# Top-query attention, routed FFN and linear attention on one core: attention's closing stage in two groups of batches, the gate layers of linear attention in four strips and three

## The chip, the cores and the metric

The kernel runs on one NeuronCore of a Trainium2 chip. Its engines are TensorE (PE: matmuls into PSUM; its weight loads are listed apart as PEld), VectorE (DVE), ScalarE (ACT), GpSimd (POOL) and SyncE (SP, which here only issues DMAs). Each runs its own instructions in order; semaphores make one wait for another. The metric is the device time of one execution in microseconds, as a median over several runs.

## The reference

All arrays are float32. The input `x` has 8 batches of 512 tokens with 256 channels. Four sublayers follow each other, each added to `x` after a layer norm:

1. Attention with 16 heads of 16 channels, in which only the 307 queries of a head with the largest sparsity count; the output of every other query is zero.
2. A routed FFN: 16 blocks of 64 hidden units, of which each token uses the 4 that a softmax router ranks highest.
3. Gated linear attention over the batch axis (8 time steps, for each of 512 tokens), with its own RMS norms and a SwiGLU FFN.
4. The routed FFN again, with the same weights.

```python
scores = einsum('bhqd,bhkd->bhqk', q, k) * scale
sparsity = scores.max(axis=-1) - scores.mean(axis=-1)
_, top_idx = top_k(sparsity, U)                 # U = int(0.6 * 512)
...
out = zeros_like(q).at[bi, hi, top_idx].set(softmax(scores_sel) @ v)
return out @ Wo + bo
```

```python
gate_hidden = silu(xb @ wg1.T + bg1)            # 256 -> 16
alpha = sigmoid((gate_hidden @ wg2.T + bg2) / GATE_TEMP)    # 16 -> 256
S = a_t[..., None] * S + k_t[..., :, None] * v_t[..., None, :]   # S is zero before step 0
o_t = einsum('bhk,bhkv->bhv', q_t, S)
```

Because the state is zero before the first step, the decay `alpha` of step 0 (batch 0) multiplies zero.

## The kernel before

The residual `xres` stays in SBUF for the whole run: 128 partitions by 8 batches by 4 token slices of 128 by 256 channels. Names with `_ps` are PSUM tiles; PSUM has eight banks of 512 floats per partition.

**Attention.** A list `steps` (L483) has 128 entries: batch `b`, head groups `m` and `e`, and one of four blocks `k` of queries or keys. Each step is done twice. `max_one` (L415) computes scores with queries on the partitions, and DVE takes their row maximum into `mx`. `exp_one` (L429), 16 steps later (`LAG`), computes the transposed scores, ACT takes the exponential, and `weigh` (L440) multiplies by the values into `av`. The loop at L539 mixes the two: in iteration `n` the maxima of step `n` (`ahead`) and the exponentials of step `n - 16` (`here`), until the maxima end at `n = 127` and 16 iterations of exponentials are left. The maxima draw from `bank_m`, a ring of four banks; the exponentials then draw from `bank`, a ring of three.

After the four blocks of one `(b, m, e)`, `place_maxima` (L396) transposes `mx` on PE, negates it on ACT and sends it with eight small DMAs of SP: four into spare rows of the queries `q`, where the second pass uses it as the softmax shift, and four into `neg`, which collects the values for the choice of queries (a head's row has one value per query). When the last maxima are there, `top_queries` (L464) copies `neg` to `work` and on DVE removes the largest values eight at a time, in 26 rounds of `max` and `match_replace`. `take` (L449) copies a finished `av` to SBUF, sends the row of softmax sums to `den` by a DMA of ACT, and POOL puts the two head halves together in `outC[b]`.

**End of attention.** At L617 DVE takes the reciprocal of `den` for all heads, and with the mask from `work` makes `nrm`: the weight of each head and query, 16 rows per batch. PE spreads these rows over the channels by multiplying with the constant `spread`; two batches share a strip of 32 rows. Four batches of the same parity stand in four different strips, and the loop at L621 takes them one after another. DVE multiplies `outC[b]` by the result (L630), 16 instructions in all. The memory of the weights that follow (`wpool`) becomes free with the end of attention; SP issues their loads then.

**Output projection and routing.** `out_projection` (L770) has four units per token slice `k`; a unit projects two batches with `wo_a` into a bank (four matmuls of 256 columns) and DVE adds it to `xres`. `route(k, ...)` (L787) is a generator: statistics of slice `k` on DVE, normalized rows on ACT, transposes on PE to `xnT`, the router's logits, softmax, the four highest, the mask's transpose `mT_ps`, and a DMA round trip that spreads the mask. The function `between` (L702) alternates units of one list with pieces of a generator. At L1192 the four units of slice 0 come first, then the twelve units of the other slices alternate with the routing of slice 0; the first FFN follows.

The kernel's source gives the order in which instructions are made; the tile framework sets the order within each engine's queue from it, and so a unit can appear in another place than in the text.

**Linear attention.** `gla(k)` (L961) handles one slice, and its pieces alternate with FFN units. Its gate has two layers. The first, `gh_ps` (L980), has 16 outputs and 1024 tokens of the slice as two groups of 512 columns, each in a strip of 32 PSUM rows; ACT applies SiLU. The second, `al_ps` (L992), takes the 16 values and a row of ones as 32 contraction rows and produces 256 decays for 128 tokens per matmul; the two groups lie in two strips of rows. Its result `al` is used by POOL and DVE. `vm` (L671) subtracts each head's mean from the value weights `q_w`, 12 short DVE instructions that stand in the source directly after the weight loads.

Of the kernel before, what the change touches and what calls it, by code (L numbers as in the profile page):

```python
# [10 lines left out]
F32 = mybir.dt.float32  # L11
# [6 lines left out]
P = 128  # L18
# [20 lines left out]
def block_kernel(ctx: ExitStack, tc: tile.TileContext, t: dict, out: bass.AP):  # L39
# [59 lines left out]
    with ExitStack() as outer:  # L99
# [21 lines left out]
        mx = a_out.tile([P, NB, NG, 4 * 4], F32, name="mx")  # L121
        work = a_out.tile([P, L + 8], F32, name="work")
        m8 = a_out.tile([P, 8], F32, name="m8")

        with ExitStack() as inner:
# [4 lines left out]
            def load_heads(name, src, eng):  # L130
                wp = load_chunked(a1, name + "_pad", src, eng)
# [264 lines left out]
            def place_maxima(b, m, e):  # L396


                q = fronts[b][0][e]
                pt = bank_m(f"mxT_ps{b}")  # L400
                nc.tensor.transpose(pt[0:16, 0:P], mx[:, b, 2 * e + m, :], ident)
                negT = a2.tile([16, P], F32, tag="negT", name=f"negT{b}")
                nc.scalar.mul(negT, pt[0:16, 0:P], -1.0)
                r = b * H + 8 * e + 4 * m
                for k in range(4):
                    nc.sync.dma_start(
                        out=q[DH * (1 - e) :: 32, m, bass.ts(k, P)],
                        in_=negT[4 * k : 4 * k + 4, :],
                    )
                for k in range(4):  # L410
                    nc.sync.dma_start(
                        out=neg[r : r + 4, bass.ts(k, P)], in_=negT[4 * k : 4 * k + 4, :]
                    )
# [68 lines left out]

            steps = [  # L483
# [54 lines left out]

            for n in range(len(steps) + LAG + 1):  # L539
                ahead = steps[n] if n < len(steps) else None  # L540
# [28 lines left out]
                if ahead is not None and ahead[3] == 3:  # L569
                    full.append((n + 2, ahead[0:3]))  # L570
                if n + 1 == len(steps):
                    place_full(n + 2)
                    top_queries()
# [22 lines left out]


# [15 lines left out]
        with tc.tile_pool(name="a_tail", bufs=2) as tail:  # L613

            nrm = tail.tile([P, L], F32, tag="nrm", name="nrm", bufs=1)
            rden = tail.tile([P, L], F32, tag="rden", name="rden", bufs=1)
            nc.vector.reciprocal(rden, den)  # L617
            nc.vector.scalar_tensor_tensor(
                nrm, work[:, 0:L][:, ::-1], REPL, rden, ALU.not_equal, ALU.mult
            )  # L620
            for u in range(2):  # L621
                for m in range(NC2):
                    for i in range(4):
                        b = 2 * i + u
                        rows = bass.ts(i, 32)
                        ps = (bank if i % 2 else bank_m)(f"nrm_ps{b}")
                        nc.tensor.matmul(
                            ps, spread[rows, u, m, :], nrm[rows, :], start=True, stop=True
                        )
                        nc.vector.tensor_tensor(  # L630
                            outC[b][:, m, :], outC[b][:, m, :], ps, ALU.mult
                        )

# [11 lines left out]
    q_wg2 = wpool.tile([64, D], F32, name="q_wg2")  # L647
    q_bg1 = wpool.tile([64, 1], F32, name="q_bg1")
    gh = wpool.tile([64, 512], F32, name="gh")
# [6 lines left out]
    for g in range(2):  # L656
        r = 32 * g + DH
        nc.sync.dma_start(out=q_wg2[32 * g : r, :], in_=t["b_wg2T"])
# [4 lines left out]
        nc.sync.dma_start(out=q_bg1[32 * g : r, :], in_=t["b_bg1c"])  # L663
# [6 lines left out]

    vm = wpool.tile([P, NC2, H], F32, name="vm")  # L671
    for c in range(NC2):
        for m in range(NC2):
# [597 lines left out]
```

## Time and profile before

| | us |
|---|---|
| median of 3 runs (1651.06 to 1651.93) | 1651.34 |
| the profiled execution, device time | 1653.55 |
| its span in the trace | 1651.8 |
| PE busy | 1599.0 (97%) |
| DVE busy | 969.4 (59%) |
| ACT busy | 671.7 (41%) |
| POOL busy | 334.3 (20%) |

A busy PE is not PE at its peak, because matmuls are pipelined and their ends are modelled. A float32 matmul appears as two records. In the profile's rows "a<-b" means that tile `a` is written from `b`; "x8" is a number of instructions; a bracket with an arrow names the idle time before an instruction and what ended it. The granted clock (PEclk) is the share of full TensorE speed.

Operations that the change touches, from the trace of this execution:

| operation | engine | count | length of one |
|---|---|---|---|
| row maximum (L425) | DVE | 512 | 0.68 us, one each 0.65 |
| exponential (L437) | ACT | 512 | 0.60 us |
| issue of a `neg` or `q` DMA | SP | 256 | 0.6 us |
| reciprocal of `den` (L617) | DVE | 1 | 3.34 us |
| multiply of `outC` (L630) | DVE | 16 | 0.68 us, one each 0.60 |
| projection unit `ao_ps` (8 records) | PE | 16 | 1.73 us at full clock |
| add of two FFN biases to `xres` (L797) | POOL | 32 | 1.27 us |
| SiLU of `gh` (L989) | ACT | 8 | 0.68 us |
| sigmoid of `al` (L1003) | ACT | 16 | 0.60 us |

### The profile page before, as it was taken

What the parts mean: (1) busy time and instruction counts of PE and PEld (TensorE: products, weight loads), DVE (VectorE), ACT (ScalarE), POOL (GpSimd) and SP (SyncE); (2) the same over time, 40 slices, a digit from 0 to 9 for tenths busy, and PEclk for the clock granted to TensorE, in tenths of its full rate; (3) what the DMA queues carried; (4) which work ended last, traced back from release to release, by engine and by line L of the source; (5) the groups of instructions that cost most, each with busy time, mean ns of one, the idle gap of its engine ahead of it and who ended that gap; (6) DMA issues with size and microseconds to landing.
All of it is one profiled execution on the core that took longest, in us unless ns stands there. A gap on an engine that the chain in (4) does not pass through costs nothing.

```text
span 1651.8 us, 19680 instructions
## 1 busy us (share of the span) xinstructions
PE 1599.0 (97%) x7378; PEld 820.1 (50%) x7378; DVE 969.4 (59%) x2015; ACT 671.7 (41%) x1208; POOL 334.3 (20%) x381
## 2 busy tenths in 40 slices
PE   7999999999999969999989999999999999999999
PEld 3323223333233237655564556555555556766666
DVE  6978776676667786447672666277355633344342
ACT  2366666665656814252346123622521352121010
POOL 3111111010000102114342442154223421000000
PEclk9999999999999979999999999999999999999999
DMA  3100000000000051010000001000000010011100
GB/s 109 40 2 3 2 2 3 2 2 3 2 3 3 2 165 26 3 37 13 1 1 0 1 1 27 0 0 1 0 1 1 0 26 1 20 33 35 43 26 26
DMA packets 24276, 27.58 MB, mean 17 GB/s; under 512 B 6229, under 2 KB 20725, under 8 KB 24181
## 3 DMA queue, kind: packets, MB, share of 16 engines
q1 hardware_dynamic: 23108, 24.75, 5.2%
q10 hardware_dynamic: 1072, 1.57, 0.3%
q8 instruction: 58, 0.95, 0.2%
q14 instruction: 38, 0.30, 0.1%
HBM read 21.20 MB, written 4.33 MB: 15 GB/s over the span
## 4 chain that ended last, share of the span: by engine, by line
PE 77%; DVE 14%; ACT 3%; POOL 3%; issue 1%; DMA 1%; SPq 0%; ACTq 0%; POOLq 0%; DVEq 0%
PE y_ps L889 16%; PE h_ps L909 11%; PE s L433 8%; PE s L422 8%; PE swi_ps L936 7%; PE proj_ps L1019 7%; PE av L442 7%; DVE pr L1052 2%; DVE pr L1042 2%; PE ao_ps L775 2%; PE q_ps L316 2%; PE gla_y L1144 2%; DVE mx L425 2%; PE v_ps L376 2%; PE k_ps L316 2%; POOL o L1069 1%
## 5 line engine op out<-in xcount | busy, mean ns | idle before, releaser
L425 DVE TENSOR_REDUCE mx<-s 128x1 f32<-128x512 f32 x512 | 329.0, 684 | 129.8 <-PE s L433 83.0
L437 ACT ACTIVATE e<-s 128x512 f32<-128x512 f32 x512 | 276.1, 599 | 179.0 <-PE s L433 103.5
L422 PE MATMUL s<-k,q 32*128 32x512 f32 x1024 | 298.9, 641 | 3.2 <-ACT k L367 2.5
L433 PE MATMUL s<-q,k 32*128 32x512 f32 x1024 | 294.3, 638 | 0.4 <-DVE mx L425 0.3
L889 PE MATMUL y_ps<-w,h 128*128 128x256 f32 x1024 | 232.9, 383 | 2.9 <-DVE h L918 2.9
L909 PE MATMUL h_ps<-xnT,w 128*128 128x512 f32 x512 | 229.8, 597 | 4.1 <-ACT h L917 4.1
L889 PEld LDWEIGHTS y_ps<-w,h 128*128 128x128 f32 x1024 | 194.1, 192 | 41.0 <-issue 10.8
L909 PEld LDWEIGHTS h_ps<-xnT,w 128*128 128x128 f32 x512 | 95.5, 191 | 113.8 <-issue 107.1
L442 PE MATMUL av<-e,va 128*32 128x512 f32 (+1 forms) x1120 | 141.9, 568 | 3.8 <-ACT e L437 2.4
L918 DVE TENSOR_TENSOR h<-h,mk 128x512 f32<-128x512 f32 x128 | 97.6, 774 | 78.9 <-ACT h L917 70.0
L917 ACT ACTIVATE h<-h_ps,b 128x512 f32<-128x512 f32 x96 | 65.6, 684 | 178.1 <-PE h_ps L909 178.0
L422 PEld LDWEIGHTS s<-k,q 32*128 32x128 f32 x1024 | 89.5, 184 | 86.0 <-DVE mx L425 56.1
L433 PEld LDWEIGHTS s<-q,k 32*128 32x128 f32 x1024 | 88.1, 183 | 80.8 <-ACT e L437 53.8
L894 DVE TENSOR_TENSOR xres<-xres,y_ps 128x512 f32<-128x512 f32 x48 | 32.8, 683 | 162.2 <-PE y_ps L889 125.0
L936 PE MATMUL swi_ps<-zT,w_gate 128*128 128x512 f32 x256 | 122.7, 599 | 4.8 <-DVE h L945 4.8
L936 PE MATMUL swi_ps<-zT,w_up 128*128 128x512 f32 x256 | 121.2, 594 | 0.0
L1019 PE MATMUL proj_ps<-q_w,rT 128*128 128x512 f32 x256 | 118.3, 601 | 0.0
L889 PE MATMUL y_ps<-w_down,h 128*128 128x256 f32 x512 | 116.8, 380 | 0.0
L889 PEld LDWEIGHTS y_ps<-w_down,h 128*128 128x128 f32 x512 | 95.7, 190 | 20.0 <-issue 8.5
L942 ACT ACTIVATE h<-swi_ps 128x512 f32<-128x512 f32 x64 | 38.2, 596 | 156.7 <-PE swi_ps L936 156.6
L1069 POOL TENSOR_TENSOR o<-o,pr 128x512 f32<-128x512 f32 (+2 forms) x56 | 80.9, 1444 | 58.9 <-DVE pr L1052 56.9
L797 POOL TENSOR_TENSOR xres<-xres,b 128x512 f32<-128x512 f32 x32 | 40.1, 1271 | 240.0 <-ACT row L737 217.7
(191 smaller groups left out, 1713.9 us busy)
## 6 DMA issues: line engine op xcount, KB each, us to landing
mk<-md SPq DMA_DIRECT2D x32, 256.0 KB
xres<-in_L_attn_a_x SPq DMA_DIRECT2D x8, 512.0 KB
out<-xres SPq DMA_DIRECT2D x16, 256.0 KB
q<-negT SPq DMA_DIRECT2D x128, 2.0 KB
neg<-negT SPq DMA_DIRECT2D x128, 2.0 KB
w<-in_f_w1T SPq DMA_DIRECT2D x1, 1024.0 KB
w<-in_f_w2T SPq DMA_DIRECT2D x1, 1024.0 KB
w_gate<-in_b_w_gateT SPq DMA_DIRECT2D x1, 1024.0 KB
```

What stands on the lines that cost most here:

```text
L316: nc.tensor.matmul(ps, w[:, c, bass.ts(m, P)], xnT[:, c, :], start=(c == 0), stop=(c == NC2 - 1),)
L422: nc.tensor.matmul(s, qs[e][rows, m, bass.ts(k, P)], ks[e][rows, m, :], start=True, stop=True)
L425: nc.vector.tensor_reduce(mx[:, b, 2 * e + m, r : r + 1], s, AX.X, ALU.max)
L433: nc.tensor.matmul(s, ks[e][rows, m, bass.ts(kt, P)], qs[e][rows, m, :], start=True, stop=True)
L437: nc.scalar.activation(ex, s, AF.Exp, scale=1.0 / DH**0.5)
L442: nc.tensor.matmul(av[32 * j : 32 * j + 32, queries], va[:, 8 * kt + 4 * m + j, e, :], es[j][:, queries], start=(kt == 0), stop=(kt == 3 a ...
L889: nc.tensor.matmul(y[0][:, bass.ts(i, D)], h[f][:, bass.ts(2 * u + i, P)], w[:, f, :], start=(f == 0), stop=(f == NF - 1),)
L909: nc.tensor.matmul(ps, w1[:, c, bass.ts(f, P)], xT[g][:, c, :], start=(c == 0), stop=(c == NC2 - 1),)
L918: nc.vector.tensor_tensor(hf, hf, mk[g][:, f, :], ALU.mult)
L936: nc.tensor.matmul(ps, w[:, c, bass.ts(f, P)], zT[g][:, c, :], start=(c == 0), stop=(c == NC2 - 1),)
L1019: nc.tensor.matmul(ps, rT[b // G4][:, c, bass.ts(b % G4, P)], q_w[:, c, m], start=(c == 0), stop=(c == NC2 - 1),)
L1069: nc.gpsimd.tensor_tensor(dst, dst, src, ALU.add)
```

## The change

**Maxima and placement.** A counter `coming` takes the place of `n` for the maxima. From `n = 112` on, every fourth iteration does the maxima of one more step, so that the last is done at `n = 124`; `top_queries` is then emitted there. `place_maxima` can take a part of the four query blocks: for the last `(b, m, e)` the first three go together and the fourth by itself. For the last batch the DMAs into `neg` are issued ahead of those into `q`.

```diff
+            coming = 0
+            def all_maxima(step):
+                nonlocal coming
+                coming += 1
+                if coming > len(steps) - 2:
+                    full.append((n + 1, step[0:3] + ((range(3), range(3, 4))[step[3] - 2],)))
+                elif step[3] == 3:
+                    full.append((n + 2, step[0:3]))
+                if coming == len(steps):
+                    place_full(n + 2)
+                    top_queries()
...
+                if ahead is not None:
+                    all_maxima(ahead)
+                    if n >= 112 and n % 4 == 0 and coming < len(steps):
+                        ahead = steps[coming]
+                        for i in range(4):
+                            max_one(*ahead, i, bank_m)
+                        all_maxima(ahead)
...
-                for k in range(4):
-                    nc.sync.dma_start(
-                        out=q[DH * (1 - e) :: 32, m, bass.ts(k, P)],
-                        in_=negT[4 * k : 4 * k + 4, :],
-                    )
-                for k in range(4):
-                    nc.sync.dma_start(
-                        out=neg[r : r + 4, bass.ts(k, P)], in_=negT[4 * k : 4 * k + 4, :]
-                    )
+                targets = [q[DH * (1 - e) :: 32, m, :], neg[r : r + 4, :]]
+                if b == NB - 1:
+                    targets = targets[::-1]
+                for target in targets:
+                    for i, k in enumerate(tiles):
+                        nc.sync.dma_start(
+                            out=target[:, bass.ts(k, P)], in_=negT[4 * i : 4 * i + 4, :]
+                        )
```

**Weights in two groups of batches, and eight projection units ahead.** `weights_of` does reciprocal and mask for the rows of some batches; two copies of one element on POOL make the reciprocal wait for the top-k's last `m8` and the mask for the last exponential. `weigh_outputs` is the old loop for some batches, with banks taken in turn. Batches 0 to 5 go first. Then come the weights of batches 6 and 7, six units of slices 0 and 1, the multiplies of batches 6 and 7, and two units of slice 2. These eight units (`out_unit`) use attention's banks; ACT copies the bank to SBUF and POOL adds it to `xres`. `out_projection` keeps the other eight, with DVE's add: one unit of slices 0 and 1 each, two of slice 2, four of slice 3.

```diff
+        def weights_of(batches, late, late_form):
+            rows = slice(16 * batches[0], 16 * batches[-1] + 16)
+            first = slice(rows.start, rows.start + 1)
+            nc.gpsimd.tensor_copy(rden[first, 0:1], late)
+            nc.gpsimd.tensor_copy(nrm[first, 0:1], late_form)
+            nc.vector.reciprocal(rden[rows, :], den[rows, :])
+            nc.vector.scalar_tensor_tensor(
+                nrm[rows, :], work[rows, 0:L][:, ::-1], REPL, rden[rows, :],
+                ALU.not_equal, ALU.mult,
+            )
+        def weigh_outputs(batches):
+            picks = itertools.cycle((bank, bank_m))
+            for u in range(2):
+                for m in range(NC2):
+                    for b in batches[u::2]:
+                        strip = bass.ts(b // 2, 32)
+                        ps = next(picks)(f"nrm_ps{b}")
+                        nc.tensor.matmul(
+                            ps, spread[strip, u, m, :], nrm[strip, :], start=True, stop=True
+                        )
+                        nc.vector.tensor_tensor(
+                            outC[b][:, m, :], outC[b][:, m, :], ps, ALU.mult
+                        )
+        def out_unit(tail, k, b):
+            y = bank(f"ao_ps{b}")
+            for i in range(2):
+                for m in range(NC2):
+                    nc.tensor.matmul(
+                        y[:, bass.ts(i, D)], outC[b + i][:, m, bass.ts(k, P)],
+                        wo_a[:, m, :], start=(m == 0), stop=(m == NC2 - 1),
+                    )
+            st = tail.tile([P, L], F32, tag="ao", name=f"ao{b}")
+            nc.scalar.copy(st, y)
+            x = xres[:, b : b + 2, k, :]
+            nc.gpsimd.tensor_tensor(x, x, st.rearrange("p (b d) -> p b d", d=D), ALU.add)
...
+            weights_of(range(NB - 2), m8[0:1, 0:1], last_exps)
...
+            weigh_outputs(range(NB - 2))
+            last = outC[NB - 3][0:1, 1, 0:1]
+            weights_of(range(NB - 2, NB), last, last)
+            for k in range(2):
+                for b in range(0, NB - 2, 2):
+                    out_unit(tail, k, b)
+            weigh_outputs(range(NB - 2, NB))
+            for b in (0, 2):
+                out_unit(tail, 2, b)
...
-        return [functools.partial(unit, b) for b in range(0, NB, 2)]
+        return [functools.partial(unit, b) for b in range((6, 6, 4, 0)[k], NB, 2)]
```

To make room for `nrm` and `rden`, the padded query and key weights are loaded into slots of the ring of the keys `k1` instead of tiles of their own.

**Gate layers.** The first layer has four strips of 256 columns instead of two of 512. The second takes the strips 1, 2, 3 together (six matmuls in three banks) and then strip 0, of which only batch 1 is computed; the unused decay of batch 0 is left out. `q_wg2`, `q_bg1` and `gh` have 128 rows instead of 64, with six more small loads on SP.

```diff
-        ps = bank_l("gh_ps")
+        ps = bank_l("gh_ps")[:, 0 : 2 * P]
         for c in range(NC2):
-            for g in range(2):
+            for u in range(G4):
                 nc.tensor.matmul(
-                    ps[bass.ts(g, 32), :], q_wg1[:, c, :], rT[g][:, c, :],
+                    ps[bass.ts(u, 32), :], q_wg1[:, c, :],
+                    rT[u // 2][:, c, bass.ts(u % 2, 2 * P)],
                     start=(c == 0), stop=(c == NC2 - 1),
                 )
...
+        for us in ((1, 2, 3), (0,)):
+            ps = [bank_l("al_ps") for u in us]
+            new = range(us[0] == 0, 2)
+            for i in new:
+                for y, u in zip(ps, us):
                     nc.tensor.matmul(
+                        y[:, bass.ts(i, D)], gh[bass.ts(u, 32), bass.ts(i, P)],
+                        q_wg2[bass.ts(u, 32), :], start=True, stop=True,
                     )
```

**`vm`.** Its twelve instructions move behind the first routed FFN, each group held by a one-element POOL copy (`hold`) of the newest FFN result.

## The prediction

> **What bounds the kernel now.** I read the page's slice rows first, then the chain of waits between 480 and 680 us, then stretches of 10 us there, then the tensor engine's (PE's) timeline. The slice rows:
>
> ```profile
> PE   7999999999999969999989999999999999999999
> PEclk9999999999999979999999999999999999999999
> ```
>
> PE is full nearly everywhere, so work that leaves PE is a gain where PE is the bound, and an idle PE is one too. One slice (the fifteenth, 578 to 619 us) stands out, in both rows. The chain there:
>
> ```profile
> 540.34 0.69 DVE mx L425
> ...
> 545.99 2.47 DMA neg<-negT
> 548.54 0.99 DVE work L468
> ...
> 589.25 3.34 DVE rden L617
> 592.67 0.66 DVE nrm L618
> 593.46 2.10 PE nrm_ps L627 x8
> 595.56 4.11 DVE outC L630 x7
> ...
> 606.25 14.98 PE ao_ps L775 x56
> ...
> 639.86 2.58 PE h_ps L909 x6
> ```
>
> Columns are start, length, engine, tile and line. The last maximum ends at 541.03; its placement lands at 548.5; 40.7 us of top-k on the vector engine (DVE) follow, up to 589.25; then reciprocal, mask, 16 multiplies, and only then the projections, all 16 of them ahead of the first FFN matmul. Attention itself (exponentials, `av`) ended at 582. What PE did meanwhile (stretch, length, busy us with counts for PE, PE's weight load, DVE, ACT, POOL, then granted clock, DMA share, GB/s):
>
> ```profile
> 570.00:580.00 10.00, 9.66 (x71) 2.79 (x68) 9.55 (x21) 9.04 (x19) 0.77 (x1) 1.00 0.01 3
> 580.00:590.00 10.00, 1.88 (x8) 0.28 (x4) 9.52 (x21) 2.65 (x4) 3.06 (x7) 0.71 0.13 16
> 590.00:600.00 10.00, 6.47 (x26) 2.39 (x26) 7.77 (x13) 0.00 (x0) 0.00 (x0) 0.60 1.07 326
> 600.00:610.00 10.00, 6.40 (x17) 3.62 (x16) 7.07 (x21) 0.00 (x0) 0.00 (x0) 0.74 0.53 159
> ```
>
> From 582 to 606 DVE is the bound, PE works 8.5 us in 24 and its clock falls. The later stretch that the change touches is the gate part of linear attention:
>
> ```profile
> 723.90 1.91 PE L983 MATMUL gh_ps<-rT,q_wg 128*32 128x512 f32 x8
> 728.10 1.99 PE L997 MATMUL al_ps<-q_wg,gh 32*128 32x256 f32 x12
> 730.64 1.13 PE L997 MATMUL al_ps<-q_wg,gh 32*128 32x256 f32 x4
> ```
>
> It stands between PE work without gaps, four times in the run.
>
> **Part 1: maxima ahead.** Iterations 112, 116 and 120 take one more step of maxima each; iterations 125 to 127 have exponentials alone. No instruction is added but a transpose. A mixed step lasts 3.66 us (14.66 for four, by the spacing of the `st` copies), an exponential-only step 2.40 (9.62 for four, ACT bound). An extra step costs PE at least 1.07 us (eight `s` records, 523.92 to 524.99). It also takes four banks of the ring of four that the maxima share, and the next maxima wait for DVE at 0.65 each; DVE has 10.3 us of maxima in 14.66, so room is there. Below 1.07 nothing can go; above, a whole step at 3.66 is the end. I take 1.6, near the PE row, because DVE drains the backlog inside the next step. Then the last maximum ends 3 x 3.66 - 3 x 1.6 = 6.2 us sooner, about 534.9, and attention ends 3 x (1.6 - 1.26) = 1.0 us later, about 583.
>
> **Part 2: placement.** The last step's tile goes by itself, `neg` first. Before, four `q` and four `neg` issues stood behind the last maximum (SP, 0.6 each) plus 2.5 to land: 7.5 us from maximum to `work`. Now SP still has the six issues of the three earlier tiles (about 533.6 to 537.2), then one issue 0.6 and 2.5 landing: `work` copy at 540.4 against 548.5, **8.1 us sooner**. The `q` issues come later, but `q` of that batch is read some 15 steps later.
>
> **Part 3: weights in two pieces.** Top-k now ends about 581 (589.25 less 8.1). The two one-element POOL copies hold the reciprocal behind the last `m8` and the mask behind the last exponential (583); behind the first copy in POOL's queue stand three `outC` operations of batch 7 (0.8 to 1.3 each), done by 584 instead of 575, which nobody needs before batch 7's weights. They also push POOL's memsets and so the weight loads on SP by 1 to 2 us; six small loads add about 4 us at SP before the gate weights. All these land before 626, needed after 640 or much later: nothing.
> Reciprocal of 96 rows: the row has 3.34 for 128 rows; fewer rows could make it 2.5, I take 3.34 (same length per row). With the last replacement (0.77) and mask (0.69), first `nrm` matmul at 585.7 against 593.46: **7.8 sooner**. First multiply 2.1 later, twelve at 0.60: the first projection's inputs are there after ten, 594.0. The `vm` work (12 instructions, 3 us at 0.17 to 0.29 each) no longer stands between the multiplies.
> The second reciprocal and mask (4 us, new) run on DVE from 595 to 601, under the first projections.
>
> **Part 4: eight projections early.** In before the first unit took 3.8 us (606.25 to its add at 610.07), the second 2.6, each later one 1.73: a slow clock, then full. Six units from 594.0: 3.8 + 2.6 + 4 x 1.73 = 13.3, so 607.3. *Clock, row and rule:* the Trainium skill ("TensorE: Matmul & The Clock Gate", "Why this matters for your kernels") says gaps up to about 3 us do not cost the clock. PE's gap shrinks from 11.6 to about 3, so by the rule all units run at 1.73, 2.9 us better. But the row above has the clock at 0.60 while PE was busy 6.5 in 10, paced by DVE as it will be again; I keep the slow start.
> Then four `nrm` matmuls of batches 6 and 7. Before, four batches sat in four row strips side by side; these two share one strip, so eight passes run one after another. *Second rule:* the same page ("The mechanism" of Part 3) lets a weight load overlap a running matmul only if the row group differs: 8 x (0.43 + 0.18) = 4.9 us. The trace's `y_ps` rows keep 0.215 apart with 0.19 loads in the same rows, so loads hide: 8 x 0.43 = 3.4 us (0.43 being half a 512-column pair, 0.86). I take 3.6, to 611. Two units more: 614.5 to 615. Each unit adds an ACT copy (0.6) and a POOL add (1.27), both shorter than the unit and on idle engines; DVE's statistics wait for POOL's adds and stand ahead of batch 6's multiply in DVE's order, about 1 us, hidden by PE's `nrm` passes.
> At 615 comes the unit for batches 6, 7 of token slice 0, on which routing of slice 0 waits. Here the gain shrinks: unit 1.7, add 0.7, statistics 1.0, so 618.5; then DVE's order has three adds or pairs of statistics of other slices (2.3) ahead of reciprocal and shift, and rows on ACT start at 621.7 against 620.34 before, **later**. But behind it PE now has 7 units instead of 12, and most statistics of slices 1 and 2 are done. Before, routing's logits waited for PE (631.56). Now they wait for ACT: eight rows at 0.5 and a copy (626.3), then in ACT's order a root and a row of slice 1, which needs DVE's shift (627.1), then the second copy (0.6): about 628.4. Softmax and top 4 took 7.9 us from transposed logits to `mT_ps` (634.4 to 642.27); one DVE add in it waits for the last unit, I take 6.7: mask transpose at 637.0 against 642.27, with 2 hidden units done in PE against 1.5 (0.86 us). Late next is this DVE chain: PE waits some 2 us for it. **Gain 5.4 + 0.9 = 6.3 us.**
>
> **Part 5: `vm` moved** behind the first FFN: 3 us on DVE in a stretch where it works 25 us in 60; its first use is at 731. Nothing; if it fell ahead of a mask multiply, up to 2 us.
>
> **Part 6: strips.** `gh`: 16 instead of 8 passes, of half the columns, four abreast instead of two: 1.91 becomes about 1.05 (four rounds of 0.215 and start), gain 0.85. Were strips not abreast, 3.4, a loss of 1.5; the logits (32 passes of 128 columns in 1.08, in four such strips) are nearest and speak for overlap. `al`: 14 passes instead of 16, three abreast, one unused block left out: four rounds of 0.76 (1.99 and 1.13, less their overlap) become three, gain 0.76. Against it: four `gh` activations of 256 for two of 0.68, about +0.35 on ACT, which the chain passes in the second of the four places. I take 1.1 net each, **4.5 us** (ends 2 and 6.4).
>
> **Sum.** 6.3 + 4.5 = 10.8 us. The profiled execution (1653.55, span 1651.8) would become 1642.8; it lies 2.2 above the median of 1651.34, which becomes **1640.5**.
>
> **Rivals.**
> - *The routing chain hides the early projections.* It starts no earlier (621.7), and DVE carries it; if it is as long as before, 6.3 falls to about 0 and the strips alone remain: 1646.8. For it: DVE is busy 8 to 9.5 in 10 there. Against: 8 adds leave DVE.
> - *PE stays slow (slower than before).* The early units are cut by waits, and the clock does not recover: eight units at 3.8 and `nrm` passes of twice the length are 8 x 3.8 + 6.9 = 37.3 us, against 13.3 + 3.6 + 3.5 = 20.4: +17, so 1657.5. It decides from about five of eight units slow (10.8 us). Against: in before two units sufficed to recover.
> - *The strips run one after another:* 1.5 lost four times, `al` no gain: 1651.3 - 6.3 + 6 = 1651.
> - An extra step of maxima priced as a full step (3.66) costs 6.2: 1646.7, held by the range.
>
> **How the numbers follow.** Forecast 0.62 (own range 1636 to 1645), hidden projections 0.20, strips serial 0.08, slow PE 0.10 (in part of it only some units are slow). Faster is the forecast, 0.19 of the second, 0.03 of the third and 0.02 of the fourth; no change 0.01, 0.05 and 0.02 of these. Uncertain terms: Part 1 from -1.6 to +6, slow start -2.9 to +3, chain 2 each way, strips 2 to 6.4. Range 1633.5 to 1648.5. 0.2% is 3.3 us, about what a measurement tells: faster 0.86, same 0.08, slower 0.06.
>
> **What would show it.** `work` copy near 540; first `nrm` matmul near 586; six `ao` units from 594; statistics' activation near 618.6; first `mT_ps` near 637; `gh_ps` groups near 1.05 us. Wrong if the three extra steps last over 6 us each, if the clock stays at 0.6 past 600, or if `mT_ps` comes at 642.

## The result, and the profile after

The changed kernel takes 1632.9 us (median of 4 runs: 1628.96, 1632.87, 1632.94, 1632.99) against 1651.49 for the kernel before: a ratio of 0.9881 with a 95% interval from 0.9869 to 0.9893. That is 18.6 us sooner. The forecast said 10.8 sooner, 1640.5, with a range down to 1633.5; the direction was right and the size was too small. A second set of runs of the same kernel, taken with the experiments, gave 1632.02 and a ratio of 0.9884 [0.9870, 0.9897]. The profiled execution is the fastest of the four (1628.96, span 1627.2), 4 us below its median, where the profiled execution of before lay 2 us above its own; differences between the two traces are therefore some 6 us too large in all.

First the page's slice rows of the changed kernel (40 slices, tenths of busy time and of granted clock):

```profile
PE   6999999999999999999989999999999999999999
PEclk9999999999999999999999999999999999999999
```

The fifteenth slice, 6 busy and 7 clock before, is now like its neighbours. The same place in stretches of 10 us (columns as before: length, busy us and counts of PE, weight loads, DVE, ACT and POOL, then granted clock, DMA share, GB/s), changed kernel:

```profile
580.00:590.00 10.00, 9.13 (x47) 2.62 (x42) 8.68 (x14) 2.79 (x6) 5.19 (x11) 1.00 0.01 2
590.00:600.00 10.00, 9.77 (x45) 8.29 (x45) 9.56 (x17) 2.92 (x5) 5.44 (x7) 1.00 0.95 289
600.00:610.00 10.00, 10.00 (x31) 6.51 (x30) 5.58 (x20) 1.23 (x3) 3.59 (x3) 0.83 0.33 78
```

PE works 28.9 us of these 30, where it worked 14.8 before. It is the bound here now; DVE, which was the bound, is hidden for most of the stretch. PE's own timeline (start, length, engine, line, operation, tiles, records; in brackets the idle time ahead and what ended it), changed kernel:

```profile
584.23 5.47 PE L147 MATMUL nrm_ps<-nrm,spread 32*128 32x512 f32 x24 [0.61 <-DVE nrm L135]
589.77 1.56 PE L160 MATMUL ao_ps<-wo_a,outC 128*128 128x256 f32 x6
591.56 9.33 PE L160 MATMUL ao_ps<-wo_a,outC 128*128 128x256 f32 x42 [0.23 <-DVE outC L150]
600.83 3.70 PE L147 MATMUL nrm_ps<-nrm,spread 32*128 32x512 f32 x8
604.45 5.40 PE L160 MATMUL ao_ps<-wo_a,outC 128*128 128x256 f32 x16
...
622.21 1.27 PE L853 MATMUL lg_ps<-xnT,rw 128*32 128x128 f32 x32
...
630.92 0.33 PE L904 MATMUL mT_ps<-ident,taken 128*128 128x128 f32 x1 [0.25 <-DVE taken L897]
```

The 11.59 us of idle time ahead of the first `nrm_ps` have become 0.61. The six early units (48 records) end at 600.83. The pair of units at 604.45 takes 5.40 instead of about 3.7: there the clock was at half speed for 3.4 us, the only such stretch of this stage. The mask's transpose, 642.27 before, comes at 630.92, and PE waits 0.25 for it.

The chain of waits of the changed kernel at the same place (start, length, what):

```profile
581.54 0.99 ACT e L485 x2
...
590.23 1.29 DVE outC L150 x2
591.56 9.33 PE ao_ps L160 x42
```

The 40 us of top-k are no longer in it; attention's last exponential and PE's work are. Between the first two lines the inferred chain goes over the last batch's sums and a small transfer, for which DVE's timeline shows no wait: its multiplies run without a break from 587.87 to 592.70. And the top-k still counts. DVE's timeline at the mask, changed kernel:

```profile
582.71 0.68 DVE L522 MATCH_REPLACE8 work<-m,work 128x520 f32<-128x520 f32 x1
583.49 0.69 DVE L135 SCALAR_TENSOR_TENSOR nrm<-work,rden 96x512 f32<-96x512 f32 x1
```

The reciprocal (579.42 to 582.77) is done ahead of the last replacement, which ends at 583.39; POOL's copy that announces the last exponential ends at 582.76. The two ways to the mask now end within 0.6 us of each other, the top-k's last.

The gates of linear attention, first of the four places, changed kernel:

```profile
711.62 1.07 PE L1030 MATMUL gh_ps<-rT,q_wg 128*32 128x256 f32 x16
715.41 1.14 PE L1047 MATMUL al_ps<-q_wg,gh 32*128 32x256 f32 x12
717.97 0.69 PE L1047 MATMUL al_ps<-q_wg,gh 32*128 32x256 f32 x2
```

`gh` went from 1.91 to 1.07, `al` from 3.12 (1.99 and 1.13) to 1.83.

### The profile page after: what moved, and what is told of

Same layout as the page of the kernel before. It is cut to its first block, busy times and chain, and to the rows that moved or that the text cites. A ratio compares the mean times of both kernels' runs of the same rounds, so it can differ in the third digit from the quotient of the medians.

```text
span 1627.2 us, 19790 instructions
## 1 busy us (share of the span) xinstructions
PE 1587.9 (98%) x7403; PEld 814.5 (50%) x7403; DVE 962.8 (59%) x2009; ACT 677.8 (42%) x1226; POOL 348.5 (21%) x397
## 4 chain that ended last, share of the span: by engine, by line
PE 77%; DVE 12%; ACT 4%; POOL 3%; issue 2%; DMA 1%; SPq 0%; ACTq 0%; POOLq 0%; DVEq 0%
PE y_ps L936 16%; PE h_ps L956 10%; PE s L481 9%; PE s L470 8%; PE av L490 8%; PE swi_ps L983 7%; PE proj_ps L1069 7%; DVE pr L1102 2%; DVE pr L1092 2%; PE q_ps L362 2%; PE gla_y L1194 2%; DVE mx L473 2%; PE v_ps L422 2%; PE k_ps L362 2%; PE chT_ps L793 2%
```

## Experiments

All medians below stand beside 1651.4 to 1651.8 us for the kernel before in the same runs; the ratio with its 95% interval decides. Gains and losses in us are differences of medians unless the ratio is named; a difference between two of the changed kernels carries the intervals of both ratios, together some 3 us.

| run | median us | ratio to before |
|---|---|---|
| after_again: the changed kernel once more | 1632.02 | 0.9884 [0.9870, 0.9897] |
| gates_only: before with the new gate layers | 1641.27 | 0.9942 [0.9929, 0.9956] |
| old_gates: changed, with the old gate layers | 1636.81 | 0.9914 [0.9901, 0.9928] |
| pe_busy: before, PE's gap filled | 1651.90 | 1.0007 [0.9999, 1.0015] |
| no_ahead: changed, no extra maxima steps | 1639.30 | 0.9925 [0.9912, 0.9937] |
| late_units: changed, no early units | 1641.97 | 0.9942 [0.9930, 0.9955] |
| gap3: changed, first weights 10 us later | 1643.92 | 0.9952 [0.9938, 0.9966] |
| ahead_only: before with the maxima ahead and their placing | 1652.62 | 1.0001 [0.9992, 1.0009] |
| ahead_vm: the same, and vm moved | 1647.88 | 0.9982 [0.9973, 0.9991] |
| vm_only: before with vm moved | 1649.80 | 0.9987 [0.9978, 0.9995] |
| vm_back: changed, vm at its old place | 1630.67 | 0.9870 [0.9857, 0.9884] |
| two_strips: changed, see below | 1628.50 | 0.9854 [0.9839, 0.9869] |
| gap1: changed, first weights 3.35 us later | 1637.05 | 0.9913 [0.9900, 0.9927] |
| al_pairs: changed, second layer in pairs of strips | 1632.90 | 0.9895 [0.9880, 0.9910] |
| gh_alone: before, first layer in four strips, second in pairs | 1643.06 | 0.9951 [0.9938, 0.9963] |
| al_twice: changed, second layer's products made twice | 1636.93 | 0.9915 [0.9902, 0.9929] |

### The two halves of the change

after_again has no edit. gates_only takes the gate part of the change over into the kernel before, old_gates takes it back out of the changed kernel:

```diff
-        ps = bank_l("gh_ps")                    # old_gates: the two hunks reversed
+        ps = bank_l("gh_ps")[:, 0 : 2 * P]
...
-        for u in range(2):
-            ps = [bank_l("al_ps") for g in range(2)]
+        for us in ((1, 2, 3), (0,)):
+            ps = [bank_l("al_ps") for u in us]
```

> The changed kernel once more. Its four runs were 1628.96 once and 1632.9 three times, all with nearly full clock. If the 4 us between them are one more stretch at half clock, this profile shows it, at 1632.9 with a mean clock of 0.994; if it is something else (DMA, the scalar engine), the clock is 0.997 and landmarks shift elsewhere.

> The kernel before with the two gate layers of the changed kernel alone. By my forecast 4.5 us (1647.0). By the records of the changed kernel, 4 x (1.91 - 1.07) for gh and 4 x (3.05 - 1.75) for al, 8.5 us (1643.0), and the closing stage of attention as before (mask transpose at 642.3). If clock falls in the later stages are what moved, anything up to 12 us.

> The changed kernel with the two gate layers of before. By the records 8.5 us above the changed kernel (1641.4); by my forecast 4.5 (1637.4). The closing stage of attention stays as changed: mask transpose near 631, 12.1 us ahead of before in the first add of the FFN.

The profile of after_again answers its question: behind the first FFN its clock was at half speed for 13.7 us, against 3.4 in the first trace, and the span is 1629.7 against 1627.2. So stretches at half speed do move the time; that they make all of the 4 us is not shown.

The gate layers alone gain 10.5 us by the medians, 9.6 by the ratio; the rest alone gains 15.0 (14.2 by the ratio). Together they give 19.8. So the gates are worth 10 alone and 4.8 on top of the rest, and the rest alone is worth more than twice the 6.3 that I had given it. Both terms were too small; they are taken apart below.

### Which parts of the attention's end carry the gain

The maxima ahead and their placing alone, in the kernel before:

```diff
+            def all_maxima(step):
...
+                    if n >= 112 and n % 4 == 0 and coming < len(steps):
+                        ahead = steps[coming]
```

> The kernel before with the maxima ahead and their placing alone: one group of weights, the projection as before. Theory A (the routing's chain starts at the top-k, and everything up to the first mixer follows it one for one): 7 to 8 us gained, 1643.5 to 1645. Theory B (without the early units the projection behind the multiplies stays the bound): also tied to the top-k, but the reciprocal's gap and slow clock stay, so not more than 8. Theory C (the last exponentials, 1 us later, hold the multiplies): 0 to 3 us gained, 1649 to 1651.5.

Nothing was gained, nearest to Theory C in size but not for its reason. DVE's timeline of ahead_only:

```profile
586.85 3.35 DVE L637 RECIPROCAL rden<-den 128x512 f32<-128x512 f32 x1 [6.97 <-POOL st L461]
...
593.15 4.28 DVE L650 TENSOR_TENSOR outC<-outC,nrm_ps 128x512 f32<-128x512 f32 x7 [2.22 <-PE nrm_ps L647]
601.03 0.29 DVE L696 TENSOR_REDUCE vm<-q_w 128x8 f32<-128x128 f32 x1 [3.60 <-DMA q_w<-in_b_wvT]
601.23 0.68 DVE L650 TENSOR_TENSOR outC<-outC,nrm_ps 128x512 f32<-128x512 f32 x1
```

The top-k ends at 579, 9 us sooner, and then DVE idles 6.97 us: the reciprocal of all 128 rows needs the last batch's softmax sums, which come with attention's end (last exponential 582, copy, a DMA, POOL). It starts 2.4 us sooner than before, not 9. Then the eighth multiply stands behind a `vm` reduction that waits 3.60 us for the value weights; these arrive after attention's end, which came no sooner (its last `av` ends at 583.4, before at 581.9). So two waits that the old top-k had hidden took its place. With `vm` moved as well:

```diff
-    vm = wpool.tile([P, NC2, H], F32, name="vm")      # ahead of the multiplies
+    vm = wpool.tile([P, NC2, H], F32, name="vm")      # behind the first routed FFN
```

> The kernel before with the maxima ahead and with vm moved, but one group of weights and no early units. In the run with the maxima ahead alone the reciprocal started 2.4 us sooner than before and the multiplies then stood 3.6 us behind a vm reduction that waited for q_w's transfer, with 2.3 us of vm work between them besides. Theory A (these two ate the gain): multiplies end 5 to 6 us sooner than in that run, 1646 to 1648. Theory B (the slow clock or the projection behind the multiplies eats it in any case): no gain, 1650.5 to 1652.5. In neither is it the 8 us by which the top-k starts sooner, since the last batch's row of sums holds the reciprocal.

> The kernel before with vm moved behind the first routing, nothing else. Theory A (vm's twelve small instructions, 2.3 us, stand between the multiplies that pace the stretch, so they are on the path): 2 to 2.5 us gained, 1649 to 1649.6. Theory B (as predicted, the step moves nothing): 1651.5 within 0.8.

> The changed kernel with vm at its place of before. By its order of instructions vm stands on VectorE between the statistics and the multiplies of batches 6 and 7. Theory A (it delays these multiplies by its 2.3 us and by what it waits for q_w's transfer, and TensorE has only two units as cover): 1 to 4 us lost, 1633.5 to 1637. Theory B (the two units cover it): within 0.8 of the changed kernel, 1631.7 to 1633.3.

In ahead_vm the sixteen multiplies run from 593.15 to 602.81 without a break, and 3.0 us are gained by the ratio: the upper edge of Theory A's times. vm_only gains 2.1 by the ratio and 1.6 by the medians, its multiplies lasting 9.66 us instead of 11.33: Theory A. In vm_back the reduction again waits for its weights (1.88 us), and ends the multiplies of batches 6 and 7 at 609.9 instead of 605.6, but PE has the two units to do until 610: no loss that the runs can tell; at 1630.67 it even lies 1.0 below the band of Theory B. So moving `vm` is worth something where DVE is the bound and nothing in the changed kernel.

The opposite, the changed kernel without the extra steps of maxima (there are three, at `n` = 112, 116 and 120; the expectation says four):

```diff
-                    if n >= 112 and n % 4 == 0 and coming < len(steps):
+                    if n >= 1000 and coming < len(steps):
```

> The changed kernel without its four extra steps of maxima; all else stays. Theory A (the start of the top-k sets the whole stretch up to the first mixer, and from the first product with the weights on TensorE is full, so a shift arrives one for one at the end): top-k starts about 8 us later, the attention's last exponential about 1 us sooner, so 7 to 8 us lost: 1639.5 to 1641. Theory B (TensorE's own work, the last exponentials and the first six batches' outputs, is late anyway, and the earlier top-k is partly hidden): 0 to 3 us lost, 1632 to 1635.

PE's timeline of no_ahead at the first product with the weights:

```profile
589.79 7.83 PE L147 MATMUL nrm_ps<-nrm,spread 32*128 32x512 f32 x24 [7.78 <-DVE nrm L135]
```

It loses 7.3 us against after_again, 6.8 by the ratio: Theory A, 0.2 below its range and far from B's. The top-k starts 4.8 us later, not 8, since the run keeps the new placing: `work` is copied 3.4 us after the last maximum, where the kernel before took 7.5. The first product comes 5.6 us later; the other 1.7 are the clock's, as is seen below. And without the early units:

```diff
-            for k in range(2):
-                for b in range(0, NB - 2, 2):
-                    out_unit(tail, k, b)
...
-            for b in (0, 2):
-                out_unit(tail, 2, b)
...
-        return [functools.partial(unit, b) for b in range((6, 6, 4, 0)[k], NB, 2)]
+        return [functools.partial(unit, b) for b in range(0, NB, 2)]
```

> The changed kernel with the weights still made for six batches and then for two, but with all 16 projection units after the last multiply and none in the attention's banks. Theory A (the eight early units fill the time in which the second reciprocal, its mask and the multiplies of batches 6 and 7 run): TensorE idles about 7 us from 590 on and meets the units with a lower clock, 7 to 10 us lost: 1639 to 1642. Theory B (the scheduler's order or the projection's own buffers hide it as in the kernel before): 0 to 2 us lost.

10.0 us are lost against after_again: Theory A, at its upper end. PE's timeline of late_units:

```profile
583.24 5.52 PE L147 MATMUL nrm_ps<-nrm,spread 32*128 32x512 f32 x24 [0.62 <-DVE nrm L135]
596.25 7.19 PE L147 MATMUL nrm_ps<-nrm,spread 32*128 32x512 f32 x8 [7.49 <-DVE nrm L135]
```

The first group is as early as in the changed kernel, but PE then stands idle for 7.49 us, under the second reciprocal and mask, and the eight products of batches 6 and 7 take 7.19 us at half clock instead of 3.70. Its ratio, 0.9942, is that of gates_only: without the early units the rest of the change at attention's end gains nothing. Of the parts, then, neither the earlier top-k nor the early units can be left out: the top-k's gain needs the group without the last batches, and that group needs the units behind it.

### The clock

In the kernel before the clock fell to 0.60 and 0.74. What lowers it? First PE's gap ahead of the first product was filled with 13 matmuls whose results are not read:

```diff
+            for i in range(13):
+                idle = (bank if i % 2 else bank_m)("idle_ps")
+                nc.tensor.matmul(idle, ident, outC[i % 6][:, 0, :], start=True, stop=True)
```

> The kernel before with 13 matmuls of 512 columns, whose results nobody reads, between the end of attention and the weights, so that the tensor engine is not idle from 582 to 593. If the idle gap is what lets the clock fall, the clock stays at 1.0 through the multiplies and the first two projection units take 1.73 instead of 3.8 and 2.6: 3 to 5 us faster (about 1647). If the clock falls anyway in the stretch that the vector engine paces (my forecast's reading of its row), no change, 1651.5.

No change in time. Stretches of pe_busy:

```profile
580.00:590.00 10.00, 10.00 (x27) 4.12 (x26) 9.52 (x21) 2.83 (x4) 3.06 (x7) 1.00 0.11 15
590.00:600.00 10.00, 8.79 (x34) 2.84 (x33) 7.45 (x12) 0.00 (x0) 0.00 (x0) 1.00 1.05 321
600.00:610.00 10.00, 6.63 (x13) 3.36 (x14) 7.65 (x21) 0.00 (x0) 0.00 (x0) 0.56 0.54 161
```

The filler keeps the clock up until 600, 0.60 before; then it falls to 0.56 all the same, in the second half of the multiplies, where PE waits for DVE again and again (no gap over 1.9 us, PE busy 6.63 in 10). The first projections meet the same slow clock. So the gap is not the only cause. Then the reverse, a gap put back into the changed kernel, by doing the first reciprocal four times or twice:

```diff
-            nc.vector.reciprocal(rden[rows, :], den[rows, :])
+            for _ in range(4 if batches[0] == 0 else 1):
+                nc.vector.reciprocal(rden[rows, :], den[rows, :])
```

> The changed kernel with its first reciprocal done four times, so that the first product with the weights comes 10 us later (three times 3.35 us) and TensorE's gap ahead of it grows from 0.6 to about 10.7 us. Theory A (the gap is what slows the clock, as it did in the kernel before): the delay and a start at half speed, 10 + 3 to 6 us lost: 1645 to 1649, and a granted clock below 0.8 in the 10 us behind the gap. Theory B (it is the stretch paced by VectorE's multiplies that slows the clock, not the gap): 10 us lost, 1642 to 1643, and the clock at 1.00 at its start.

> The changed kernel with its first reciprocal done twice: TensorE's gap ahead of the first product with the weights grows from 0.6 to about 4 us. Gaps of 7.7, 7.8, 10.6 and 11.6 us stood ahead of a clock of 0.50 in other runs, one of 0.6 did not. Theory A (a gap of 4 us is already enough): 3.4 us of delay and about 1.5 for the clock, 1637 to 1638, with a granted clock of 0.6 to 0.9 from 590 to 600. Theory B (4 us leave the clock as it is): 1635.3 to 1636.5, clock at 1.00 up to 600.

PE's timeline of gap1 at the first product, and two stretches:

```profile
587.81 7.63 PE L148 MATMUL nrm_ps<-nrm,spread 32*128 32x512 f32 x24 [3.98 <-DVE nrm L136]
...
590.00:600.00 10.00, 10.00 (x33) 6.08 (x28) 9.65 (x15) 0.58 (x1) 0.69 (x3) 0.59 0.90 274
600.00:610.00 10.00, 10.00 (x41) 7.41 (x40) 8.15 (x25) 2.92 (x5) 7.21 (x6) 1.00 0.43 94
```

A gap of 3.98 us is enough: 0.59 in the ten microseconds that follow it, although PE is never idle in them; the record has 10.2 us at half speed from 588.0. In the seven traces with the early units and a gap of 0.6 us (both of the changed kernel, old_gates, vm_back, two_strips, al_pairs, al_twice) there is at most one stretch of 3.4 us up to 610. Theory A for gap1, 5.0 us lost against after_again for 3.35 of delay. With 10.6 us of gap, in gap3, the clock is 0.50 from 590 to 600 and 0.63 from 600 to 610, Theory A's clock, and the loss is 11.9 for 10.05 of delay: the clock costs less than A said. By the medians the slow start costs 1.7 to 1.9 us in three kernels (no_ahead, gap1, gap3), with the wide interval said above. Their traces need 48.5, 48.0 and 49.3 us from the first product to the mask's transpose, the changed kernel 46.7: 1.3 to 2.6 us, not the 3 to 6 that gap3's expectation had. One reason is that the changed kernel pays for one half-speed stretch of 3.4 us itself (at 604.5 in one trace, at 589.1 in the other; al_pairs, whose trace has none in this stage, needs 45.0), and these three have none behind their slow start.

### The gate layers

> The changed kernel with the decays' second layer in two strips at a time and all sixteen passes, the first layer in four strips. Theory A (TensorE is the bound in all four places, so its records add up: 3.05 against 1.80 us, four times): 5 us lost, 1637 to 1638. Theory B (in some of the four places something else is the bound, as the 4.8 us measured for both layers together against 8.2 by the records suggests): 2 to 3.5 us lost, 1634 to 1636.

> The kernel before with the first layer in four strips alone, the second in two. Theory A (1.91 becomes 1.07 four times, as predicted): 3.4 us gained, 1647.5 to 1648.5. Theory B (the strips also take away half-speed stretches of the clock in later stages, which would be why both layers alone gave 10 us): 5 us or more gained, below 1646.5.

> The changed kernel with the second layer's products made twice over into the same bank, the second time with the same values. By the records of its 12 and 2 passes this is about 1.3 us more of TensorE in each place. Theory A (TensorE is the bound in all four places): 5.2 us lost, 1637 to 1638. Theory B (not in all of them): 2 to 4 us lost, 1634.5 to 1636.5. An effect over 6 us would say that sparse products cost clock beyond their own time.

```diff
-        for us in ((1, 2, 3), (0,)):
+        for us in ((1, 2), (3, 0)):           # al_pairs, gh_alone
...
-            for i in new:
+            for i in [*new, *new]:            # al_twice
```

al_twice loses 4.9 us against after_again, for 5.2 by its records: nearest Theory A, that TensorE is the bound in all four places, though the interval takes in part of Theory B (its trace decides below). al_pairs loses nothing that the runs can tell, below what both theories said, because the expectation was wrong about what the edit does. PE's timeline of al_pairs, first place:

```profile
714.00 1.15 PE L1047 MATMUL al_ps<-q_wg,gh 32*128 32x256 f32 x12
716.14 1.13 PE L1047 MATMUL al_ps<-q_wg,gh 32*128 32x256 f32 x4
```

The first 12 passes take 1.15, as with three strips, not the 1.99 of the old kernel. The second pair uses other strips than the first, so the two pairs can overlap; only the last four passes, 1.13 for 0.69, are longer. So about two thirds of the second layer's gain in this place (0.84 of 1.29 us) come from the first layer's layout, four strips of rows instead of two; taking three at a time and leaving out the unused block give the other 0.45. For the same reason gh_alone does not size the first layer alone, and its 8.1 us (by the ratio) are nearly the 9.6 of both: its Theory B is not shown by its time.

How much of this is the strips' work and how much the clock's, the distance between the first and the last addition of an FFN product to `xres` shows; between them only the strips differ, and `vm` on DVE. It is 985.9 us in the trace of before, 975.0 in gates_only, 973.6 and 977.5 in the two traces of the changed kernel, 982.7 in old_gates. The half-speed stretches in it add up to 17.1, 6.8, 3.4, 13.7 and 10.2 us. With half of these taken off, since PE is the bound, the old strips give 977.3 and 977.6 and the new ones 971.6, 971.9 and 970.7: by this estimate **the strips themselves are worth 6.0 us**, in whatever surrounding, and most of the rest of the scatter is stretches of half speed at 1.7 us each. The other traces, taken the same way, agree: 977.0 to 978.9 with the old strips, 971.3 to 972.7 with the new. al_twice has 977.1, so its doubled passes cost their full 5.2 us, and TensorE is the bound in all four places. The two runs with pairs have 974.6 and 972.6, on average 1.7 above the new strips, as their records say (1.8). The new strips have fewer: behind the first FFN 14.2 us on average in the six traces with old gates and 8.2 in the twelve with new ones. One of them lies directly behind the fourth place. Stretches of 5 us there, kernel before:

```profile
1190.00:1195.00 5.00, 5.00 (x24) 3.16 (x22) 0.00 (x0) 4.22 (x6) 0.62 (x1) 1.00 0.00 0
1195.00:1200.00 5.00, 5.00 (x9) 2.13 (x9) 0.29 (x1) 1.07 (x2) 1.55 (x3) 0.66 0.00 0
```

The old `al` passes end at 1195.15 and the clock falls to 0.66, with PE busy throughout. It is there in four of the six traces with old gates and in none of the twelve with new ones. That the strips cause this is likely, not shown.

### A version that may be faster still

PE is full from 584 to 640, and two things on it can be shortened: the products of batches 6 and 7 in one strip (3.70 us), and the half-speed stretch behind them. ScalarE copies the 32 weight rows to partitions 0 to 31, so that two strips are used, and one unit moves ahead:

```diff
-            weigh_outputs(range(NB - 2, NB))
-            for b in (0, 2):
-                out_unit(tail, 2, b)
+            nc.scalar.copy(nrm[0:32, :], nrm[P - 32 :, :])
+            out_unit(tail, 2, 0)
+            weigh_outputs(range(NB - 2, NB), (3, 0))    # strip 3 for m = 0, strip 0 for m = 1
+            out_unit(tail, 2, 2)
```

> The changed kernel with the weights of batches 6 and 7 copied by ScalarE to partitions 0 to 31, so that half of their four products with spread go to a second row strip, and with one projection unit moved ahead of them. Theory A (TensorE is full from 584 to 640 us, so each us off its work comes off the time): their 3.70 us become about 1.9, and if the half-speed stretch at 604.5 goes too, another 1.7: 1.5 to 3.5 us gained, 1629 to 1631.2. Theory B (another wait, the multiplies on VectorE or the copy, takes its place): no gain, 1632 to 1633.5.

1628.5 us, 3.5 below the changed kernel's second set of runs: Theory A by its sign. The two were not timed side by side; the intervals of their ratios, up to 0.9869 and from 0.9870, only just do not meet. Against vm_back, a changed kernel that was timed beside it, it is 2.2 us, and there the intervals overlap. PE's timeline of two_strips:

```profile
602.72 1.99 PE L147 MATMUL nrm_ps<-nrm,spread 32*128 32x512 f32 x8
604.64 1.99 PE L160 MATMUL ao_ps<-wo_a,outC 128*128 128x256 f32 x8
607.37 7.61 PE L822 MATMUL ao_ps<-wo_a,outC 128*128 128x256 f32 x34 [0.73 <-DVE outC L150]
```

The eight products take 1.99, the unit behind them 1.99 at full clock, and a new wait of 0.73 for the last multiply is what remains. From the first product to the mask's transpose this trace needs 44.3 us, the changed kernel 46.7. But al_pairs, which edits nothing in this stage, has 45.0, since its trace has no half-speed stretch there. So some 0.7 to 1.0 us belong to the edit; whether it also removes the half-speed stretch is not shown.

## Why the prediction was right or wrong

**Part 1 (maxima ahead): right, sizes off.** The last maximum ended at 536.29, predicted 534.9: 4.7 us sooner, not 6.2, so an extra step costs 2.1 us, not 1.6. Attention's last `av` ended 1.7 later, not 1.0.

**Part 2 (placement): right mechanism, right landmark by luck.** `work` was copied at 539.84, predicted 540.4. SP's six earlier issues ended at 538.1, not 537.2; but the last transfer landed 1.1 us after its issue, not 2.5. The step from the last maximum took 3.6 us, not 5.5, which made up for Part 1.

**Part 3 (two groups): right in its order, its time put 1.5 us too late.** The reciprocal of 96 rows took 3.35, as taken; the first product came at 584.23, not 585.7. `work` was there 0.6 sooner than predicted, and its copy lasted 0.43 instead of 0.98. From the top-k's last maximum to the first product it is 5.1 us as before: the reciprocal now runs ahead of the last replacement, but the replacement then stands between it and the mask. What Part 3 passed over, and ahead_only showed, is that the old reciprocal could not have used the earlier top-k: without the first group of batches nearly all of the 8 us are lost.

**Part 4 (early units): the step that failed.** It said that PE's gap "shrinks from 11.6 to about 3" and "I keep the slow start". The gap was 0.61, since attention ended later (583.6) and the weights came sooner than I had put them; the clock stayed at 1.00 until 600 (in the second trace one stretch of 3.4 us at 589.1 was at half speed). The Trainium skill's rule that I had weighed against the row ("TensorE: Matmul & The Clock Gate", "Why this matters for your kernels": no idle gaps over about 3 us between bursts) was the better guide: behind 3.98 us the clock was at half speed for 10.2 us, behind 0.6 us for 3.4 at most. But it does not cover everything, as the clock in pe_busy fell with no gap over 1.9. Where the time was (us), against the prediction and against no_ahead, which has the slow start:

| from the first product on | predicted | changed | no_ahead |
|---|---|---|---|
| to the tenth multiply | 8.3 | 7.3 | 8.2 |
| to the end of six units | 13.3 | 9.3 | 11.8 |
| products of batches 6 and 7 | 3.6 | 3.6 | 3.6 |
| two units | 3.5 to 4 | 5.4 | 3.7 |
| to the router's logits | 13.6 | 12.4 | 12.4 |
| sum | 42.7 | 38.0 | 39.8 |

The clock made 3.4 us of the difference (the first two rows, no_ahead against changed), of which a half-speed stretch took 1.7 back in the two units. Another 2.8 were sized too long even for a slow clock: six of the first unit's eight records run ahead of its last input, and the chain of statistics, rows and transposes was 1.2 shorter. With the 1.5 of Part 3 the logits came at 622.2 instead of 628.4. From there the prediction held: 8.7 us to the mask's transpose, predicted 8.6, with two units of cover; only the 2 us that PE was to wait for it became 0.25, as PE was full. So the first FFN addition came 12.1 us sooner in the profile (13.6 in the second trace, 0.9 of it from a half-speed stretch 20 us into the run that this trace lacks) instead of 6.3. The second rule that I had weighed (same page of the skill), on loads in the same rows, was rightly set aside: eight passes took 3.70, not 4.9. Two small slips of the working changed nothing: PE's work from 582 to 606 was 9.1 us in the kernel before, not 8.5, and 642.27 less 637.0 is 5.3, not 5.4.

**Part 5 (`vm`): right for the changed kernel** (vm_back). Where DVE is the bound, in the kernel before, it would have been 2.1.

**Part 6 (strips): right mechanism, mis-sized.** `gh` gained 0.84, predicted 0.85; `al` gained 1.29 in the first place, predicted 0.76. I had counted three rounds of 0.76, where 12 passes took 1.14 and the last two 0.69. In the second and fourth place, with other products between the passes, both layers together gained 1.5 and 1.3. The whole is 6.0 at equal clock where the sum had 4.5, and the fewer half-speed stretches behind it, some 3 us on average by the estimate above, were in no term.

**The rivals.** Neither did the routing chain hide the projections, nor did PE stay slow, nor did the strips run one after another. An extra step of maxima cost 2.1 us, between the 1.6 taken and the rival's 3.66.

What stays open: why the half-speed stretches of later stages come in some traces and not in others, which is likely much of why the times of one kernel spread by some 4 us.

## What to carry to other kernels

When a chain is made to end sooner, look for what it had been hiding: here the last batch's sums and the value weights, both tied to attention's end, took all of 9 us until the work was split so that most of it did not need them. Where PE is freed of a wait, work out the new gap with care: here one of 0.6 us left the clock up but for one short stretch at most, and one of 4 us halved it for 10 us. And small products are worth laying out over all four strips of rows: here 12 passes took 1.99 us in two strips, and 1.14 to 1.15 in four, in threes or in pairs.

## What the runs showed of the hardware

- The records of the granted clock have only full and half speed here, the half-speed stretches 3.41 us long or multiples of it, but for a last one at the end of each trace. One in work that fills PE costs 1.7 us (two units took 5.40 instead of 3.7). They come also where PE is busy without a break (0.66 behind the `al` passes, 0.83 behind the one-strip products).
- A mask operation on 32 rows of 512 took 1.40 us in the changed kernel while POOL's addition ran (596.47 to 597.74), and 0.69 in two_strips with POOL idle, as on 96 and 128 rows.
- A reciprocal takes 3.35 us for 32, 96 or 128 rows of 512.
